# Joins of phases in a one-core graph kernel: the first head's rows kept on chip, row statistics taken at the close of a layer, graph products in pairs of groups

## The chip, the cores and the metric

The kernel runs on one core of a Trainium2 chip. The metric is the device time of one execution in microseconds (us). Every run that is quoted here is in the fast of the two states in which executions can fall. The engines are called as the profile calls them: PE (matrix products), PEld (loads of PE's stationary operand), DVE (VectorE), ACT (ScalarE), POOL (GpSimd), SP (the engine that issues most transfers). A name with a q is an engine's sequencer or its transfer queue.

## The reference

4096 nodes with 256 features; `adj` is a symmetric 0/1 matrix with ones on its diagonal. Layer 0 is graph attention with 4 heads, layer 1 two steps of a diffusion. Cut to what matters:

```python
def layer0(x, adj, W, a, gamma, beta):            # on relu(layernorm(x))
    h = (x @ W).reshape(n, heads, head_dim)
    e = leaky_relu(src[:, :, None] + dst.T[None])  # rank one per head, alpha 0.2
    attn = softmax(where(adj > 0, e, -9e15))
    out = einsum('nhm,mhd->nhd', attn, h)
    return layernorm(out) * gamma + beta

def layer1(X, S, ...):                            # on relu(layernorm(x)), S = adj
    R = (S + I) / rowsum
    for n in range(2):
        A = top_p_attention(Xa)                    # softmax rows cut to their 0.9 nucleus
        Xf, Xa = R @ Xf, A @ Xa
        Z = Z + Xf @ U1[n].T + Xa @ U2[n].T
    return layernorm(X + Z) * ln_g + ln_b

x = x + layer0(relu(layernorm(x)), adj, ...)
x = x + layer1(relu(layernorm(x)), adj, ...)
```

In this case's inputs gamma and ln_g are ones, and beta and ln_b are zeros. The kernel does not use that.

## The kernel before

Five phases follow each other. (1) The operand phase: per block of 128 rows the layer norm, x @ W, and bf16 operands for all heads, which are stored to DRAM. (2) Sixteen attention passes, four groups of eight row blocks times four heads: signs on ACT, masks on DVE, products on PE; a pass of the first head follows each group, and in it and in the pass before it eight row blocks are "closed" (normalised, gamma, beta, x). (3) The rows are read back, normalised and split in two for exact products with adj ("hops": R @ Xf, twice). (4) The first and (5) the second diffusion step, 32 row blocks each, software-pipelined over several blocks: exponentials on ACT, a search for the nucleus' threshold on DVE and POOL, transposes and products on PE. Last comes a repair of the rows that the fast search did not settle.

The parts that the change touches:

```python
# (1) operand phase, per group g of four row blocks
for i in range(4):
    ...
    nc.scalar.dma_start(uv_d[:, :, b].rearrange("h p t w -> p h t w"), parts)
for i in range(4):
    nc.gpsimd.tensor_tensor(x4[:, i, :], x4[:, i, :], beta_r, ALU.add)
nc.sync.dma_start(xb_d[ts(g, 4)].rearrange("b p d -> p b d"), x4)
# ... [cut]
# (2) closing of row block b
def close(i):
    b = ig * G0 + i
    xb = l0s.tile([P, D], F32, name="xb")
    nc.sync.dma_start(xb, xb_d[b])
    ob = l0s.tile([P, D], F32, name="ob")
    nc.scalar.activation(ob, o[:, i, :], AF.Identity, scale=..., bias=...)
    nc.vector.tensor_mul(ob, ob, gamma_r)
    nc.vector.tensor_add(xb, xb, ob)
    nc.sync.dma_start(x1_d[b], xb)
# ... [cut]
# (3) rows back, then one group of four row blocks after the other
for g in range(NB // 4):
    nc.scalar.dma_start(X[:, ts(g, 4), :], x1_d[ts(g, 4)].rearrange("b p d -> p b d"))
    for i in range(4):
        moments_of(mv[:, i, :], X[:, 4 * g + i, :])
    rs, nmr = steps(mv, 4, rr)
    for i in range(4):
        nc.scalar.activation(X[:, b, :], X[:, b, :], AF.Relu, scale=rs[:, i:i + 1], bias=nmr[:, i:i + 1])
        split(hl[0][:, b], X[:, b, :])
# ... [cut]
# (5) end of a row block in the second step
nc.gpsimd.tensor_tensor(r.x1, r.x1, ln_b_r, ALU.add)
nc.vector.tensor_add(hb, r.acc[:, 1, :], r.part)
normalized(hb, hb)            # DVE moments, POOL rs = (var + eps) ** -0.5, DVE rows
nc.vector.tensor_mul(hb, hb, ln_g_r)
nc.vector.tensor_add(hb, hb, r.x1)
# ... [cut]  the order in which one turn of the pipeline is traced
second_probe(blocks[b + 1])   # a pass of DVE over 4096 columns, then a chain on POOL
candidates(r, found)          # DVE
first_step(blocks[b + 2])     # a chain on POOL
third_probe(blocks[b + 1])    # a pass of DVE over 4096 columns
finish(blocks.pop(b - 2))     # the lines above
masked(r)                     # a pass of DVE over 4096 columns
```

## Time and profile before

| what | kernel before |
|---|---|
| time | 3629.36 us, median of 3 runs (3628.36 to 3630.86) |
| span of the profiled run, mean granted clock | 3626.4 us, 0.928 |
| busy share PE, PEld, DVE, ACT, POOL | 85, 68, 76, 55, 33% |
| first masks / last evacuation of the attention passes | 160.07 / 956.18 us |
| first graph product / end of the last group of them | 999.59 / 1473.67 us |
| turn of the pipeline in the second step | 28.21 to 28.23 us |

How to read it: most engines are busy in the mean, but no engine bounds the whole. What a change is worth is read from the joins, where all engines wait for one thing, and from the steady turns, where the longest engine's cycle counts. "First masks" is the start of ACT's first sign operation in the attention passes; "last evacuation" is the start of the last time that ACT takes a pass's sums from PE's accumulators. One turn of the pipeline finishes one row block, and a "probe" is one of DVE's passes over 4096 columns. In all views a line of instructions has its start, its length, the engine and line of the program, the operation, out<-in with shapes, and in brackets how long the engine had been idle before and what ended that.

### The profile page before, as it was taken

What the parts mean: (1) busy time and instruction counts of PE and PEld (TensorE: products, weight loads), DVE (VectorE), ACT (ScalarE), POOL (GpSimd) and SP (SyncE); (2) the same over time, 40 slices, a digit from 0 to 9 for tenths busy, and PEclk for the clock granted to TensorE, in tenths of its full rate; (3) what the DMA queues carried; (4) which work ended last, traced back from release to release, by engine and by line L of the source; (5) the groups of instructions that cost most, each with busy time, mean ns of one, the idle gap of its engine ahead of it and who ended that gap; (6) DMA issues with size and microseconds to landing.
All of it is one profiled execution on the core that took longest, in us unless ns stands there. A gap on an engine that the chain in (4) does not pass through costs nothing. (4 is left out here: it accounts for less than half of the span.)

```text
span 3626.4 us, 52748 instructions
## 1 busy us (share of the span) xinstructions
PE 3073.0 (85%) x19243; PEld 2460.8 (68%) x19243; DVE 2745.2 (76%) x5073; ACT 2008.7 (55%) x3180; POOL 1193.6 (33%) x2236
## 2 busy tenths in 40 slices
PE   4499898989599999848999999998489999999973
PEld 2399797989578888625676767685266666666762
DVE  6589898989665555229999999971399999899963
ACT  4588786878431100266666666633666666666521
POOL 3100000000010000048897554530475555555510
PEclk7699999999899999969999999999689999999986
DMA  9827456382154545100000000001000000000002
GB/s 274 259 84 195 163 143 210 94 234 76 49 175 163 163 163 164 45 1 9 17 15 18 15 17 15 17 18 56 1 11 21 18 18 18 23 19 18 18 20 29
DMA packets 212144, 278.26 MB, mean 77 GB/s; under 512 B 18720, under 2 KB 168864, under 8 KB 211872
## 3 DMA queue, kind: packets, MB, share of 16 engines
q1 hardware_dynamic: 162416, 214.45, 18.2%
q0 software_dynamic: 16896, 33.56, 5.1%
q10 hardware_dynamic: 32560, 26.75, 2.3%
q8 instruction: 157, 2.57, 0.3%
q14 instruction: 115, 0.94, 0.1%
HBM read 230.16 MB, written 78.09 MB: 85 GB/s over the span
## 5 line engine op out<-in xcount | busy, mean ns | idle before, releaser
L768 PE MATMUL acc<-X,eT 128*128 128x256 f32 x4160 | 999.9, 384 | 27.2 <-ACT eT L762 27.2
L768 PEld LDWEIGHTS acc<-X,eT 128*128 128x128 f32 x4160 | 761.1, 191 | 148.1 <-ACT eT L762 61.0
L281 PE MATMUL acc<-ut,m 128*128 128x195 bf16 (+1 forms) x8192 | 729.6, 249 | 84.8 <-DVE m L269 40.8
L281 PEld LDWEIGHTS <-m 128*128 128x128 bf16 x8192 | 703.3, 98 | 111.0 <-DVE m L269 56.5
L262 ACT ACTIVATE g<-sr,d_big 128x1024 bf16<-128x1024 f32 x512 | 550.2, 1178 | 50.2 <-DVE m L268 36.9
L611 ACT ACTIVATE void<-e,c 128x2048 int8<-128x2048 f32 x256 | 516.3, 2017 | 1.0
L423 PE MATMUL racc<-hl,ar 128*128 128x512 f32 x2048 | 470.0, 392 | 45.8 <-DMA at<-adj_d 41.1
L604 ACT ACTIVATE e<-mm,nm 128x1024 f32<-128x1024 f32 x256 | 284.0, 1112 | 385.7 <-PE mm L466 385.4
L423 PEld LDWEIGHTS racc<-hl,ar 128*128 128x128 f32 x2048 | 387.4, 189 | 128.2 <-POOL nmr L136 41.3
L760 PE MATMUL tp<-ident,e 128*128 128x128 f32 x2080 | 329.3, 285 | 154.9 <-DVE e L698 120.3
L760 PEld LDWEIGHTS tp<-ident,e 128*128 128x128 f32 x2080 | 251.9, 145 | 285.6 <-issue 152.1
L762 ACT COPY eT<-tp 128x512 f32<-128x512 f32 x520 | 304.1, 587 | 215.4 <-PE tp L760 215.4
L268 DVE TENSOR_TENSOR m<-g,ax 128x2048 bf16<-128x2048 bf16 x256 | 312.0, 1219 | 46.3 <-ACT g L262 42.7
L677 DVE MAX8 cand<-big 128x8 f32<-128x256 f32 x1024 | 340.3, 409 | 0.0
L466 PE MATMUL mm<-kT,qT 64*128 64x512 f32 x1024 | 286.5, 663 | 62.5 <-ACT e L604 52.1
L269 DVE TENSOR_TENSOR m<-ax,m 128x2048 bf16<-128x2048 bf16 x256 | 313.6, 1225 | 26.2 <-DVE m L268 0.5
L645 DVE SCALAR_TENSOR_TENSOR junk<-e,lowered 128x4096 uint8<-128x4096 f32 x64 | 286.1, 4471 | 55.9 <-POOL lowered L627 55.9
L419 DVE CAST ar<-at 128x1024 fp32r<-128x1024 bf16 x256 | 177.3, 693 | 192.4 <-PE racc L423 187.4
L666 DVE SCALAR_TENSOR_TENSOR big<-e,lowered 128x4096 f32<-128x4096 f32 x64 | 286.7, 4480 | 16.0 <-POOL lowered L627 16.0
L698 DVE SCALAR_TENSOR_TENSOR e<-e,found 128x4096 f32<-128x4096 f32 x64 | 286.7, 4480 | 0.0
L432 ACT ACTIVATE xf<-xf,rinv 128x256 f32<-128x256 f32 x64 | 32.7, 510 | 392.4 <-DVE xf L431 392.4
L466 PEld LDWEIGHTS mm<-kT,qT 64*128 64x128 f32 x1024 | 87.7, 196 | 177.6 <-issue 96.1
(230 smaller groups left out, 3288.4 us busy)
## 6 DMA issues: line engine op xcount, KB each, us to landing
at<-adj_d SPq DMA_DIRECT2D x256, 256.0 KB, 2.8
ut<-uv_d SPq DMA_DIRECT2D x64, 784.0 KB, 4.3
ax<-in_adj_t_dram POOLq DMA_DIRECT2D x32, 1024.0 KB, 13.5
adj_d<-ax SPq DMA_DIRECT2D x32, 1024.0 KB, 11.1
uv_d<-parts ACTq DMA_DIRECT2D x32, 392.0 KB, 9.6
xf<-xf_d SPq DMA_DIRECT2D x65, 128.0 KB, 2.0
sr<-s_d SPq DMA_DIRECT2D x16, 512.0 KB, 4.8
xf_d<-xf ACTq DMA_DIRECT2D x64, 128.0 KB, 2.2
```

Source lines behind the costliest of these rows:

```text
L262: nc.scalar.activation(g[:, c, :], shared[k].sr, AF.Relu, scale=BIG, bias=d_big[:, h, j:j + 1])
L268: nc.vector.tensor_tensor(m[0], g, a, ALU.min)
L269: nc.vector.tensor_tensor(m[1], a, m[0], ALU.subtract)
L281: nc.tensor.matmul(shared[k].acc[i][:, t, :cols], m[t][:, c, ts(i, P)], shared[k].ut[j // QUARTER][:, j % QUARTER, t, :cols], start=(j == ...
L423: nc.tensor.matmul(acc[i].rearrange("p s d -> p (s d)"), ar[:, c, ts(i, P)], hl[hop][:, j].rearrange("p s d -> p (s d)"), start=(j == 0), ...
L466: nc.tensor.matmul(pm[:, h, :], q[ts(h, DA), :], kT[ts(h, DA), ts(c, 512)], start=True, stop=True)
L611: nc.scalar.activation(void, r.e[:, ts(h, N // 2)], (AF.Relu, AF.Sign)[i], bias=r.c1, scale=-1.0, accum_out=r.sums[:, h, 2 + i:3 + i])
L666: nc.vector.scalar_tensor_tensor(big, r.e, r.c3, r.e, ALU.is_le, ALU.mult, accum_out=r.L)
L677: nc.vector.max(cand[:, s, :], big[:, ts(s, N // SEG)])
L760: nc.tensor.transpose(pt[:, i, :], r.e[:, ts(4 * g + i, P)], ident)
L762: nc.scalar.copy(eT, pt)
L768: nc.tensor.matmul(r.acc[:, 0, :], eT[:, i, :], cur[:, j, :], start=(j == 0), stop=(j == NB - 1))
```

## The change

Its intent is to close the holes between phases: fewer bytes and no reload at the first join; the statistics of finished rows early, so that they can be read back and used while the last eight blocks are closed; and two groups of graph products that take the rows of those eight blocks last. In the second step the normalisation is cut in three pieces, spread over two turns.

```diff
-            beta_r = row_vector(beta, "beta_r", l0w)
+    beta_r = row_vector(beta, "beta_r")              # gamma_r likewise: no longer in layer 0's memory
...
+        ut0 = [quarter() for q in range(4)]          # pool of these tiles opened before the operand phase
...
+                    nc.gpsimd.tensor_copy(ut0[b // QUARTER][:, b % QUARTER], parts[:, 0])
                     nc.scalar.dma_start(uv_d[:, :, b].rearrange("h p t w -> p h t w"), parts)
-                for i in range(4):
-                    nc.gpsimd.tensor_tensor(x4[:, i, :], x4[:, i, :], beta_r, ALU.add)
-                nc.sync.dma_start(xb_d[ts(g, 4)].rearrange("b p d -> p b d"), x4)
...
-                    nc.sync.dma_start(xb, xb_d[b])
+                    nc.sync.dma_start(xb, x[ts(b, P), :])
...
                     nc.vector.tensor_mul(ob, ob, gamma_r)
+                    nc.gpsimd.tensor_tensor(xb, xb, beta_r, ALU.add)
                     nc.vector.tensor_add(xb, xb, ob)
                     nc.sync.dma_start(x1_d[b], xb)
+                    moments_of(mv[:, i, :], xb)
+                    if i == G0 - 1:
+                        steps(mv, G0, l0s, x_rs[:, ts(ig, G0)], x_nmr[:, ts(ig, G0)])
...
-            mv = rr.tile([P, 4, nc.vector.BN_AGGR_DIM], F32, name="mv4", bufs=2)
-            for i in range(4):
-                moments_of(mv[:, i, :], X[:, 4 * g + i, :])
-            rs, nmr = steps(mv, 4, rr)
...
+            for ig in range(0, NB // IG, 2):
+                accs = [[psr.tile(...) for i in range(IG)] for g in range(2)]
+                late = (NB - G0) // JG if ig == 0 else NB // JG
+                for first, last in ((0, late), (late, NB // JG)):
+                    for g in range(2):
+                        part(hop, ig + g, accs[g], first, last)
+                        if last == NB // JG:
+                            close_rows(hop, ig + g, accs[g])
+                    if ig > 0:
+                        break
...
                 if b + 2 < NB:
                     first_step(blocks[b + 2])
+                if b > 2:
+                    finish_scale(blocks[b - 3])      # POOL: x1 + ln_b, then the two operations of rs
                 if b + 1 < NB:
                     third_probe(blocks[b + 1])
                 if b > 1:
-                    finish(blocks.pop(b - 2))
+                    finish(blocks[b - 2])            # DVE: sum and moments
+                if b > 2:
+                    finish_rows(blocks.pop(b - 3))   # DVE: rows, ln_g, x1
                 masked(r)
```

Cut: pools and names, the reload of the first 24 row blocks put on SP's queue instead of ACT's, the loops of the graph products moved into two functions, the calls in the repair and at the end (three blocks' pieces together).

More of the change, by code (lines that the diff above doesn't have):

```diff
@@ L98, in gat_then_top_p_diffusion @@
     ln_b_r = row_vector(ln_b, "ln_b_r")
+    gamma_r = row_vector(gamma, "gamma_r")
+    beta_r = row_vector(beta, "beta_r")
     w31_s = const.tile([P, KC, 3, DA], F32, name="w31_s")
@@ L107, in gat_then_top_p_diffusion @@
             nc.scalar.dma_start(w2_s[ts(j, DA), i, :], w2_t)
-    rinv = keep.tile([P, NB], F32, name="rinv")
+    rinv, x_rs, x_nmr = (keep.tile([P, NB], F32, name=x) for x in ("rinv", "x_rs", "x_nmr"))
     xa_d = dram.tile([NB, P, D], F32, name="xa_d")
@@ L129, in normalized, with steps @@
         nc.vector.tensor_scalar(dst, src, mv[:, 0:1], rs, ALU.subtract, ALU.mult)
-    def steps(mv, n, pool):
-        rs, nmr = (pool.tile([P, n], F32, name=x, bufs=2) for x in (f"rs{n}", f"nmr{n}"))
+    def steps(mv, n, pool, rs=None, nmr=None):
+        if rs is None:
+            rs, nmr = (pool.tile([P, n], F32, name=x, bufs=2) for x in (f"rs{n}", f"nmr{n}"))
         nc.gpsimd.tensor_scalar(rs, mv[:, :, 1], EPS, None, ALU.add)
@@ L153, in gat_then_top_p_diffusion @@
     s_d = dram.tile([H, N], F32, name="s_d")
-    xb_d = dram.tile([NB, P, D], F32, name="xb_d")
     adj_d = dram.tile([NB, P, N], BF16, name="adj_d")
-    with tc.tile_pool(name="l0", bufs=1) as l0, tc.tile_pool(name="l0a", bufs=9) as l0a:
-        gamma_r = row_vector(gamma, "gamma_r", l0)
+    with tc.tile_pool(name="l0", bufs=1) as l0, tc.tile_pool(name="l0a", bufs=9) as l0a, \
+            tc.tile_pool(name="l0u", bufs=6) as l0u:
         sd_c = l0.tile([P, 2, H, NB], F32, name="sd_c")
@@ L169, in gat_then_top_p_diffusion, with quarter @@
         ax = []
+        QUARTER = NB // 4
+        def quarter():
+            return l0u.tile([P, QUARTER, 2, W3 + 1], BF16, name="ut")
+        ut0 = [quarter() for q in range(4)]
         with tc.tile_pool(name="l0r", bufs=3) as rows, tc.tile_pool(name="l0w", bufs=1) as l0w, \
                 tc.tile_pool(name="ps2", bufs=2, space=PSUM) as ps2:
-            beta_r = row_vector(beta, "beta_r", l0w)
             a_r = row_vector(a, "a_r", l0w)
@@ L232, in gat_then_top_p_diffusion @@
                 nc.scalar.activation(e, e, AF.Exp)
-        with tc.tile_pool(name="l0m", bufs=3) as l0m, tc.tile_pool(name="l0u", bufs=6) as l0u, \
+        with tc.tile_pool(name="l0m", bufs=3) as l0m, \
                 tc.tile_pool(name="l0s", bufs=2) as l0s, tc.tile_pool(name="l0o", bufs=1) as l0o, \
@@ L237, in gat_then_top_p_diffusion @@
             PAIRS = NB // 2
-            QUARTER = NB // 4
             passes = [(ig, h) for ig in range(NB // G0) for h in range(H)]
@@ L251, in weighted @@
             def weighted(k, q):
-                ut = l0u.tile([P, QUARTER, 2, W3 + 1], BF16, name="ut")
+                ut = quarter()
                 nc.sync.dma_start(ut, uv_d[passes[k][1], :, ts(q, QUARTER)])
@@ L348, in sign_stage @@
                         sources(0)
-                        weighted(0, 0)
-                        weighted(0, 1)
+                        shared[0].ut = ut0
                     gs[n] = signs(k, p)
@@ L359, in mask_stage @@
                         nq = k * 4 + p // 4 + 2
-                        if nq < 4 * len(passes):
+                        if 4 <= nq < 4 * len(passes):
                             if nq % 4 == 0:
@@ L391, in gat_then_top_p_diffusion @@
     X = xp.tile([P, NB, D], F32, name="X")
-    with tc.tile_pool(name="rx", bufs=1) as rx, tc.tile_pool(name="ra", bufs=3) as ra, \
-            tc.tile_pool(name="rr", bufs=1) as rr, tc.tile_pool(name="psr", bufs=2, space=PSUM) as psr:
+    with tc.tile_pool(name="rx0", bufs=1) as rx0, tc.tile_pool(name="ra", bufs=3) as ra, \
+            tc.tile_pool(name="rr", bufs=1) as rr, tc.tile_pool(name="rx1", bufs=1) as rx1, tc.tile_pool(name="psr", bufs=2, space=PSUM) as psr:
         def split(dst, src):
@@ L399, in split @@
             nc.vector.tensor_tensor(dst[:, 1, :], src, dst[:, 0, :].bitcast(F32), ALU.subtract)
-        hl = [rx.tile([P, NB, 2, D], F32R, name=f"hl{i}") for i in range(2)]
+        hl = [rx.tile([P, NB, 2, D], F32R, name=f"hl{i}") for i, rx in enumerate((rx0, rx1))]
         for g in range(NB // 4):
-            nc.scalar.dma_start(X[:, ts(g, 4), :], x1_d[ts(g, 4)].rearrange("b p d -> p b d"))
-            mv = rr.tile([P, 4, nc.vector.BN_AGGR_DIM], F32, name="mv4", bufs=2)
-            for i in range(4):
-                moments_of(mv[:, i, :], X[:, 4 * g + i, :])
-            rs, nmr = steps(mv, 4, rr)
+            (nc.sync if g < 6 else nc.scalar).dma_start(X[:, ts(g, 4), :], x1_d[ts(g, 4)].rearrange("b p d -> p b d"))
@@ L408, in gat_then_top_p_diffusion @@
             for i in range(4):
                 b = 4 * g + i
-                nc.scalar.activation(X[:, b, :], X[:, b, :], AF.Relu, scale=rs[:, i:i + 1], bias=nmr[:, i:i + 1])
+                nc.scalar.activation(X[:, b, :], X[:, b, :], AF.Relu, scale=x_rs[:, b:b + 1], bias=x_nmr[:, b:b + 1])
                 split(hl[0][:, b], X[:, b, :])
-        for hop in range(STEPS):
-            for ig in range(NB // IG):
-                acc = [psr.tile([P, 2, D], F32, name=f"racc{i}") for i in range(IG)]
-                for jg in range(NB // JG):
-                    at = ra.tile([P, JG, IG * P], BF16, name="at", bufs=6)
-                    nc.sync.dma_start(at, adj_d[ts(jg, JG), :, ts(ig, IG * P)].rearrange("c p i -> p c i"))
-                    ar = ra.tile([P, JG, IG * P], F32R, name="ar")
-                    nc.vector.tensor_copy(ar, at)
-                    for c in range(JG):
-                        j = jg * JG + c
-                        for i in range(IG):
-                            nc.tensor.matmul(acc[i].rearrange("p s d -> p (s d)"), ar[:, c, ts(i, P)],
-                                             hl[hop][:, j].rearrange("p s d -> p (s d)"),
-                                             start=(j == 0), stop=(j == NB - 1))
-                for i in range(IG):
-                    b = ig * IG + i
-                    both = rr.tile([P, 2, D], F32, name="both")
-                    nc.vector.tensor_tensor(both, acc[i], hl[hop][:, b].bitcast(F32), ALU.add)
-                    xf = rr.tile([P, D], F32, name="xf")
-                    nc.vector.tensor_tensor(xf, both[:, 0, :], both[:, 1, :], ALU.add)
-                    nc.scalar.activation(xf, xf, AF.Copy, scale=rinv[:, b:b + 1])
-                    nc.scalar.dma_start(xf_d[hop][b], xf)
-                    if hop + 1 < STEPS:
-                        split(hl[hop + 1][:, b], xf)
@@ new lines, in part @@
+        def part(hop, ig, acc, first, last):
+            for jg in range(first, last):
+                at = ra.tile([P, JG, IG * P], BF16, name="at", bufs=6)
+                nc.sync.dma_start(at, adj_d[ts(jg, JG), :, ts(ig, IG * P)].rearrange("c p i -> p c i"))
+                ar = ra.tile([P, JG, IG * P], F32R, name="ar")
+                nc.vector.tensor_copy(ar, at)
+                for c in range(JG):
+                    j = jg * JG + c
+                    for i in range(IG):
+                        nc.tensor.matmul(acc[i].rearrange("p s d -> p (s d)"), ar[:, c, ts(i, P)],
+                                         hl[hop][:, j].rearrange("p s d -> p (s d)"),
+                                         start=(j == 0), stop=(j == NB - 1))
@@ new lines, in close_rows @@
+        def close_rows(hop, ig, acc):
+            for i in range(IG):
+                b = ig * IG + i
+                both = rr.tile([P, 2, D], F32, name="both")
+                nc.vector.tensor_tensor(both, acc[i], hl[hop][:, b].bitcast(F32), ALU.add)
+                xf = rr.tile([P, D], F32, name="xf")
+                nc.vector.tensor_tensor(xf, both[:, 0, :], both[:, 1, :], ALU.add)
+                nc.scalar.activation(xf, xf, AF.Copy, scale=rinv[:, b:b + 1])
+                nc.scalar.dma_start(xf_d[hop][b], xf)
+                if hop + 1 < STEPS:
+                    split(hl[hop + 1][:, b], xf)
@@ new lines, in gat_then_top_p_diffusion @@
+        for hop in range(STEPS):
+            for ig in range(0, NB // IG, 2):
+                accs = [[psr.tile([P, 2, D], F32, name=f"racc{i}") for i in range(IG)] for g in range(2)]
+                late = (NB - G0) // JG if ig == 0 else NB // JG
[6 more added lines that the diff above has]
+                        break
@@ L748, in loads @@
     def loads(r):
-        r.xf, r.part = rows.tile([P, D], F32, name="xf"), rows.tile([P, D], F32, name="part")
+        r.xf, r.part = rows.tile([P, D], F32, name="xf"), rows.tile([P, D], F32, name="part", bufs=3)
         nc.sync.dma_start(r.xf, block(xf_d[r.n], r.b))
@@ L752, in loads @@
             nc.sync.dma_start(r.part, block(z_d, r.b))
-            r.x1 = rows.tile([P, D], F32, name="x1")
+            r.x1 = rows.tile([P, D], F32, name="x1", bufs=3)
             nc.sync.dma_start(r.x1, block(x1_d, r.b))
@@ L843, in again @@
         finish(r)
+        finish_scale(r)
+        finish_rows(r)
     def repaired(n, kT, qT, nm, cur, found):
@@ L895, in finish, with finish_scale, finish_rows @@
         else:
-            nc.gpsimd.tensor_tensor(r.x1, r.x1, ln_b_r, ALU.add)
-            hb = rows.tile([P, D], F32, name="hb", bufs=1)
-            nc.vector.tensor_add(hb, r.acc[:, 1, :], r.part)
-            normalized(hb, hb)
-            nc.vector.tensor_mul(hb, hb, ln_g_r)
-            nc.vector.tensor_add(hb, hb, r.x1)
-            nc.sync.dma_start(block(out.rearrange("(b p) d -> b p d", p=P), r.b), hb)
+            nc.vector.tensor_add(r.part, r.acc[:, 1, :], r.part)
+            r.mv = small.tile([P, 1, nc.vector.BN_AGGR_DIM], F32, name="mv1")
+            moments_of(r.mv[:, 0, :], r.part)
+    def finish_scale(r):
+        if r.n + 1 == STEPS:
+            nc.gpsimd.tensor_tensor(r.x1, r.x1, ln_b_r, ALU.add)
+            r.rs = col("rs")
+            nc.gpsimd.tensor_scalar(r.rs, r.mv[:, :, 1], EPS, None, ALU.add)
+            nc.gpsimd.tensor_tensor(r.rs, r.rs, mhalf, ALU.pow)
+    def finish_rows(r):
+        if r.n + 1 == STEPS:
+            nc.vector.tensor_scalar(r.part, r.part, r.mv[:, 0, 0:1], r.rs, ALU.subtract, ALU.mult)
+            nc.vector.tensor_mul(r.part, r.part, ln_g_r)
+            nc.vector.tensor_add(r.part, r.part, r.x1)
+            nc.sync.dma_start(block(out.rearrange("(b p) d -> b p d", p=P), r.b), r.part)
     for n in range(STEPS):
@@ L947, in gat_then_top_p_diffusion @@
             finish(r)
+            for b in range(NB - 3, NB):
+                finish_scale(blocks[b])
+            for b in range(NB - 3, NB):
+                finish_rows(blocks[b])
         repaired(n, kT, qT, nm, cur, found)
```

## The prediction

> **What bounds the kernel now.** I read the page, then the busy time by stretch, then the time-ordered instructions at each join of two phases. The page gives a span of 3626.4 us with PE 85% busy, so no single engine explains it; the stretches do. (Columns: stretch, length, busy us of PE, PEld, DVE, ACT, POOL, then granted PE clock, DMA share, GB/s.)
>
> ```profile
> 10.00:150.00 140.00, 67.55 (x193) 43.11 (x193) 86.39 (x235) 70.83 (x196) 48.11 (x101) 0.71 1.04 284
> 163.00:956.00 793.00, 727.04 (x8165) 701.00 (x8166) 700.19 (x723) 630.74 (x774) 30.16 (x35) 0.98 0.49 141
> 958.00:1000.00 42.00, 0.94 (x8) 0.73 (x6) 19.94 (x61) 11.29 (x27) 5.32 (x11) 0.56 0.40 127
> 2634.00:3500.00 866.00, 777.98 (x3747) 584.53 (x3747) 788.94 (x1674) 508.31 (x756) 468.16 (x984) 0.95 0.06 19
> ```
>
> The first stretch, where layer 0's operands are made, is full on DMA (share 1.04) with DVE at 62%. The second, the attention passes, has PE and DVE both near 90%. The third is a hole: PE works 0.94 us of 42. The last is the second diffusion step, with DVE at 91%. The waits of the first stretch say what DMA holds up: a new operand buffer is not free until an old one's store has landed.
>
> ```profile
> POOL parts L211 <- DMA uv_d<-parts: 64.3, 17, 7.6
> ```
>
> Next the two joins, in order of time (start, length, engine, line, out<-in, count, idle before it and what ended that):
>
> ```profile
> 149.16 0.37 ACTq L219 DMA_DIRECT2D uv_d<-parts  x1
> 160.07 5.30 ACT L262 ACTIVATE g<-sr,d_big 128x1024 bf16<-128x1024 f32 x5 [11.78 <-DMA uv_d<-parts]
> ...
> 163.67 0.32 PE L281 MATMUL acc<-ut,m 128*128 128x196 bf16 x1 [19.52 <-DMA ut<-uv_d]
> ```
>
> ```profile
> 961.35 1.78 DVE L300 TENSOR_TENSOR st<-st 128x1560 f32<-128x1560 f32 x1 [8.01 <-ACT st L296]
> ...
> 987.62 2.70 ACTq L403 DMA_DIRECT2D X<-x_d  x4
> ...
> 999.59 1.62 PE L423 MATMUL racc<-hl,ar 128*128 128x512 f32 x3 [41.06 <-DMA at<-adj_d]
> ```
>
> First join: the last store, issued at 149.16, lands only near 160, and the first masks wait for it. Second join: DVE and ACT close the last eight row blocks from 961 to 988; only then are the rows read back, normalised and split, and PE starts at 999.6.
>
> **What the Trainium skill says.** (1) "SBUF — State Buffer", section "SBUF: two separate sides": VectorE and GpSimd share a port pair under an exclusive lock; a VectorE operation with two SBUF inputs, against a GpSimd operation that reads SBUF, holds it for its whole length. The trace of before agrees: below, a POOL operation that elsewhere takes 0.26 us takes 4.02 under the 4.48 us probe. (2) "DMA: Bandwidth & Descriptors", section "Issuing engines are not separate DMA queues": all queues run on the same 16 DMA engines. The full share of the first stretch with 64.3 us of waiting for stores agrees, so a store taken off one queue helps another. (3) "TensorE: Matmul & The Clock Gate", section on the HAM clock gate: after idling PE starts at half rate for some microseconds. Here the first eight graph products take 3.75 us, 0.47 each, and 443 per 100 us (0.226 each) later.
>
> **The change, part by part.**
>
> *First head's rows on chip, and no copy of x plus beta in DRAM.* Gone from the first stretch: eight stores of 512 KB (4.2 MB). Over its first 100 us this queue moved 12.65 MB in 38.2% of the 16 engines' time, 3.0 us per MB, so 12.7 us of DMA. On POOL 32 additions of 0.73 us go and 32 copies of about that come, a wash. With the share at 1.04 and the compute of a block (2.1 to 2.4 us between blocks near 34 to 40 us, against 3.7 on average) well below it, I take 10 of the 12.7. At the first join four loads of 784 KB of the first head are gone; three of them were in flight with the last store. That store should land in 5 us rather than 11: 6 more. The masks still wait for it, so not all 11.8. Sum -16.
>
> *Row statistics at the close of layer 0.* Each close gets a bn_stats and a bn_aggr on DVE. In the second step the same pair behind an add starts its parts 0.46 us apart, so about 0.67 us per block. The passes that close rows are DVE-bound: the pass from 346.45 to 410.66 (64.2 us between evacuations, 46.1 elsewhere) has 52.4 us of DVE work plus 11.6 of DVE waits, nearly all of it, while PE idles 11. So 24 closes x 0.67 = +16 there. About 4.6 is given back, because DVE now arrives later at waits such as this one, whose end is fixed by a DMA queue that stands behind another transfer:
>
> ```profile
> 397.50 0.42 DVE L335 TENSOR_TENSOR xb<-xb,ob 128x256 f32<-128x256 f32 x1 [6.01 <-DMA xb<-xb_d]
> ```
>
> The addition of beta on POOL (0.73 us, later if DVE holds the ports) now follows such a load: +3 to 4 over three closings. Sum +15.
>
> *The second join.* Rows 0 to 23 were stored long before, and their statistics now exist. Their loads need only X's memory, free after the last evacuation (961.3; gamma, which kept it until 987.6, has moved). A first load took 4.3 us (987.62 to 991.96), then relu, cast and split take about 2: PE starts near 968, 32 earlier. That asks that ACT and DVE take this work between the closing's instructions. The order of before allows it: in this view an instruction traced after the second step's blocks (L850) stands inside the last block's search:
>
> ```profile
> 3494.55 0.19 DVE L691 TENSOR_SCALAR work<-drop 128x48 f32<-128x48 f32 x1
> 3494.65 0.18 DVE L850 TENSOR_TENSOR failed<-found,found 128x32 f32<-128x32 f32 x1
> 3494.77 0.21 DVE L692 CUSTOM_DVE_ANT_0 work<-best,work 128x48 f32<-128x48 f32 x1
> ```
>
> ACT makes a block in 0.9 us (relu 0.55, cast 0.35), the pace at which PE eats one (4 x 0.226). DVE has 0.72 us per block (split 0.37, half a cast 0.35) beside 20 us of closing, 37 us from 965, so the first group's 24 blocks end near 1000. The second group's 24 (21.7 us) follow at full rate and cover the last eight rows. Then 1000 + (2048 - 96) x 0.226 = 1441, against 1474 in before: -33. Two groups that end 7.2 us apart need their accumulators emptied at about 3.1 us per block, so the third group waits 1 to 2 us in each hop: +3. Sum -30.
>
> *The normalisation of the second step in three pieces.* This is meant to take away DVE's wait of 1.84 us per block, some 29 blocks, 53 us. I think it takes nothing:
>
> ```profile
> 3020.13 4.48 DVE L666 SCALAR_TENSOR_TENSOR big<-e,lowered 128x4096 f32<-128x4096 f32 x1
> 3020.72 4.02 POOL L627 TENSOR_SCALAR lowered<-lowered,c 128x1 f32<-128x1 f32 x1
> ...
> 3024.70 0.19 POOL L639 TENSOR_TENSOR yy<-a 128x1 f32<-128x1 f32 x1
> 3024.85 0.55 POOL L640 TENSOR_TENSOR up<-z,mone 128x1 f32<-128x1 f32 x1
> 3025.45 0.18 DVE L124 BATCH_NORM_AGGREGATE mv<-st 128x2 f32<-128x6 f32 x1
> 3025.50 0.26 POOL L641 TENSOR_SCALAR up<-up,sg 128x1 f32<-128x1 f32 x1
> 3025.71 0.73 POOL L896 TENSOR_TENSOR x<-x,ln_b_r 128x256 f32<-128x256 f32 x1
> 3026.53 0.25 POOL L126 TENSOR_SCALAR ve<-mv 128x1 f32<-128x1 f32 x1
> 3026.87 0.57 POOL L128 TENSOR_TENSOR rs<-ve,mhalf 128x1 f32<-128x1 f32 x1
> 3027.47 0.41 DVE L129 TENSOR_SCALAR hb<-hb,mv,rs 128x256 f32<-128x256 f32 x1 [1.84 <-POOL rs L128]
> ```
>
> POOL is locked out during the probe and then runs the rest of the step's arithmetic, the addition of ln_b, and the two operations of rs without a pause. The moments are ready at 3025.63, 0.9 us before POOL reaches them at 3026.53: they aren't what it waits for. The change makes the moments a block older but leaves POOL's order (arithmetic, addition, two operations) and DVE's order (three, three, mask) as they were, so rs still comes 2.9 us after the probe and DVE still waits 1.84. The period of 28.23 us stays: 0. At the end three blocks' rows are finished together behind one chain on POOL: +1.6.
>
> Total: -16 + 15 - 30 + 0 + 1.6 = -29, so 3629.4 - 29 = 3600 us.
>
> **Rivals.** *The split normalisation works.* For: it names the longest regular wait on DVE, and PE's own cycle is 26.19 us (step one's steady period), so DVE's 26.39 would count. Against: POOL's unbroken row above. It would make 3629 - 29 - 53, about 3547. *The second join isn't interleaved*: ACT and DVE finish the closing first. For: the closing was written in a fixed order. Against: L850. PE would then start near 989 and the change would give about 3620. *The first stretch doesn't shrink*, if the buffers' round trip and not the bytes sets its pace: about 3610. *DVE in the passes hides the statistics*: no PE or DVE slack speaks for it; 3585.
>
> **Range and chances.** My terms are uncertain by 7 (first stretch), 6 (passes) and 10 us (second join), 14 together: 3572 to 3624 holds it 8 times in 10. Over 2% faster is below 3557, which needs the first rival: 0.09. Within 2%: 0.9. Slower by over 2% has no source that I can see: 0.01.
>
> **What would show it.** In the changed kernel: first masks near 144; no xb_d store; the passes with closings 4 to 5 us longer; first graph product near 967 (968, moved by the -16 and +15 of the first two terms) POOL, not DMA, ahead of some xb additions; the last graph product some 30 us earlier relative to the closing; in the second step a DVE wait of about 1.8 us for POOL's rs in every block at a period of 28.2. If that period is 26.4, the step "POOL's order sets rs" is wrong, and with it the total.

## The result, and the profile after

The changed kernel takes 3600.27 us, median of 4 runs (3595.79 to 3604.97), against 3630.11 (3628.36 to 3631.09); ratio 0.9918, 95% interval 0.9901 to 0.9936. A ratio here is the mean time of one kernel's fast runs over that of the other's of the same rounds, so not quite the ratio of the medians quoted. The result is correct in all runs.

The time came out where it was predicted, with a range that held it. Whether the reasons were right is another question. The first profile happens to be of the slowest of the four runs, so the account below uses two profiles (the second is that of the experiment after_again).

Busy time by stretch, the stretches that answer to three of those of before (stretch, length, busy us of PE, PEld, DVE, ACT, POOL, granted clock, DMA share, GB/s):

```profile
10.00:142.00 132.00, 64.71 (x193) 41.30 (x193) 82.99 (x232) 69.33 (x193) 43.47 (x99) 0.75 1.01 274
156.00:954.00 798.00, 730.34 (x8161) 701.30 (x8162) 719.03 (x770) 630.48 (x773) 67.02 (x71) 0.98 0.48 137
2611.00:3475.00 864.00, 772.09 (x3759) 580.67 (x3760) 790.37 (x1673) 507.80 (x755) 477.04 (x984) 0.96 0.06 19
```

The operand phase is still full on DMA (1.01). In the passes DVE has 19 us more work than before and POOL 37. The second step looks the same: 790 us of DVE work there, 789 before.

The first join, in order of time:

```profile
145.16 0.37 ACTq L227 DMA_DIRECT2D uv_d<-parts  x1
152.46 1.15 ACT L266 ACTIVATE g<-sr,d_big 128x1024 bf16<-128x1024 f32 x1 [8.17 <-DMA uv_d<-parts]
```

The last store is issued 4.0 us earlier than before and is waited for 7.3 us after its issue, where it was 10.9. The second join:

```profile
959.68 1.78 DVE L304 TENSOR_TENSOR st<-st 128x1560 f32<-128x1560 f32 x1 [8.00 <-ACT st L300]
...
967.78 1.62 PE L426 MATMUL racc<-hl,ar 128*128 128x512 f32 x3 [10.93 <-issue]
```

PE starts the graph products 8 us after DVE begins the last closing (38 us before).

What DVE waited for in the passes (engine, what for, us in total, times, longest), from the view of waits from 250 to 960 us. Before:

```profile
DVE xb L335 <- DMA xb<-xb_d: 16.7, 4, 7.8
```

After:

```profile
DVE xb L340 <- POOL xb L339: 1.2, 2, 0.6
```

One turn of the second step, after:

```profile
2994.05 3.98 POOL L645 TENSOR_SCALAR lowered<-lowered,c 128x1 f32<-128x1 f32 x1
...
2999.01 0.74 POOL L923 TENSOR_TENSOR x<-x,ln_b_r 128x256 f32<-128x256 f32 x1
...
2999.84 0.25 POOL L925 TENSOR_SCALAR rs<-mv 128x1 f32<-128x1 f32 x1
3000.18 0.57 POOL L926 TENSOR_TENSOR rs<-rs,mhalf 128x1 f32<-128x1 f32 x1
...
3000.78 0.41 DVE L930 TENSOR_SCALAR part<-part,mv,rs 128x256 f32<-128x256 f32 x1 [1.85 <-POOL rs L926]
```

DVE waits 1.85 us for rs, as it did before, although the moments that rs needs are now a whole turn old. The turn is 28.21 to 28.24 us.

The account, from the starts of instructions in the profiled runs (us, after minus before):

| stretch | predicted | first profile | second profile |
|---|---|---|---|
| start to first masks | -16 | -7.6 | -6.3 |
| first masks to last evacuation (796.1 before) | +15 | +5.9 | +5.8 |
| last evacuation to end of the graph products (517.5) | -30 | -29.0 | -26.9 |
| projections, up to the first masked block of step one (171.5) | 0 | +5.9 | +1.1 |
| from there to the last masked block of step two (1853.6) | 0 | -4.3 | -5.8 |
| tail with the repair (127.7) | +1.6 | +5.8 | +6.2 |
| sum | -29 | -23 | -26 |

### The profile page after: what moved, and what is told of

Same layout as the page of the kernel before. It is cut to its first block, busy times and chain, and to the rows that moved or that the text cites. A ratio compares the mean times of both kernels' runs of the same rounds, so it can differ in the third digit from the quotient of the medians.

```text
span 3603.2 us, 52704 instructions
## 1 busy us (share of the span) xinstructions
PE 3070.6 (85%) x19243; PEld 2455.2 (68%) x19243; DVE 2753.2 (76%) x5073; ACT 2008.2 (56%) x3180; POOL 1237.2 (34%) x2252
## 5 line engine op out<-in xcount | busy, mean ns | idle before, releaser
L285 PEld LDWEIGHTS <-m 128*128 128x128 bf16 x8192 | 703.9, 98 | 112.8 <-DVE m L273 65.6
L426 PE MATMUL racc<-hl,ar 128*128 128x512 f32 x2048 | 470.6, 391 | 16.3 <-issue 10.9
```

The costliest lines, as they stand in the source:

```text
L285: nc.tensor.matmul(shared[k].acc[i][:, t, :cols], m[t][:, c, ts(i, P)], shared[k].ut[j // QUARTER][:, j % QUARTER, t, :cols], start=(j == ...
L426: nc.tensor.matmul(acc[i].rearrange("p s d -> p (s d)"), ar[:, c, ts(i, P)], hl[hop][:, j].rearrange("p s d -> p (s d)"), start=(j == 0), ...
```

## The experiments

Twelve runs were made; all gave correct results. Each was timed against the kernel before in the same rounds. Where a difference lies below the spread of the times (the changed kernel's runs spread over 9 us), the verdict is taken from the starts of instructions in the trace, one profile each.

| run | us, median | ratio to before (95%) |
|---|---|---|
| pool_first | 3550.17 | 0.9781 (0.9768 to 0.9794) |
| no_add | 3574.03 | 0.9846 (0.9832 to 0.9859) |
| split_alone | 3628.59 | 0.9995 (0.9982 to 1.0009) |
| rs_before_add | 3628.45 | 0.9996 (0.9980 to 1.0013) |
| stats_alone | 3628.30 | 0.9996 (0.9982 to 1.0010) |
| no_beta_add | 3594.50 | 0.9897 (0.9880 to 0.9913) |
| store_back | 3608.24 | 0.9944 (0.9927 to 0.9960) |
| reload_head | 3601.65 | 0.9918 (0.9901 to 0.9934) |
| both_back | 3607.82 | 0.9934 (0.9917 to 0.9950) |
| one_group | 3615.93 | 0.9956 (0.9940 to 0.9973) |
| stats_at_reload | 3615.51 | 0.9957 (0.9941 to 0.9974) |
| after_again | 3602.37 | 0.9919 (0.9902 to 0.9936) |

The kernel before had medians of 3630.51 (the first four: pool_first, no_add, split_alone, stats_alone), 3631.26 (store_back, reload_head, one_group, no_beta_add) and 3631.04 (the others). The first four ran on another chip than the other eight; these medians show no difference between the two.

### The second step: does POOL's order set rs?

**pool_first.**

```diff
+                if b > 2:
+                    finish_scale(blocks[b - 3])
                 if b + 2 < NB:
                     first_step(blocks[b + 2])
-                if b > 2:
-                    finish_scale(blocks[b - 3])
                 if b + 1 < NB:
                     third_probe(blocks[b + 1])
```

> The changed kernel with one move: GpSimd's three operations for the final normalisation (the addition of ln_b and the two of rs) are traced before the first search step of the block after next, and not behind it. Theory of the prediction (GpSimd's order sets rs: it is locked out by the probe and has its arithmetic ahead of rs): rs is ready before the probe, VectorE's wait of 1.84 us per block in the second step goes, the period falls from 28.23 to about 26.4 us, and 29 blocks x 1.84 = 53 us less than the changed kernel: about 3547 us, 0.977 of the kernel before. Rival (the moments, or a wait of the program that does not depend on the order, hold the rows up): period stays 28.2, 3600 us. Second rival: the arithmetic of the search then comes 1.6 us later, and its result is waited for: period between 27 and 28.

Measured: 3550.17 us. The turn is 26.33 to 26.35 us, and the view of what DVE waited for between 2700 and 3350 us has no line left. One turn, in order of time:

```profile
2985.48 0.73 POOL L923 TENSOR_TENSOR x<-x,ln_b_r 128x256 f32<-128x256 f32 x1
...
2986.30 0.24 POOL L925 TENSOR_SCALAR rs<-mv 128x1 f32<-128x1 f32 x1
...
2986.62 0.57 POOL L926 TENSOR_TENSOR rs<-rs,mhalf 128x1 f32<-128x1 f32 x1
...
2988.11 4.48 DVE L684 SCALAR_TENSOR_TENSOR big<-e,lowered 128x4096 f32<-128x4096 f32 x1
...
2988.14 4.62 POOL L654 TENSOR_SCALAR L<-L,c,sums 128x1 f32<-128x1 f32 x1
```

The operations for rs end 0.9 us before the probe begins. What the probe now locks out (an operation of about 0.4 us that lasts 4.62) is the arithmetic of a block two turns ahead, for which nobody waits yet. This is the theory's prediction to within 0.1 us of the turn and 3 us of the time, so the step "POOL's order sets rs" is shown. It also beats both kernels.

**no_add.**

```diff
-            nc.gpsimd.tensor_tensor(r.x1, r.x1, ln_b_r, ALU.add)
```

> The changed kernel without GpSimd's addition of ln_b (right all the same, as ln_b is zero in this case's inputs), order unchanged. Theory (rs waits behind a queue of work on GpSimd that starts when the probe ends): the queue is 0.8 us shorter, so VectorE's wait falls from 1.84 to about 1.0 us and the period from 28.23 to 27.4 us, 24 us less than the changed kernel, about 3577. Rival (rs waits for the moments or for a semaphore round trip): nothing changes, 3600.

Measured: 3574.03 us. The wait totals 27.1 us in 24 turns between 2700 and 3350 us, 1.1 each; the turn is 27.51 us. So rs stands behind a queue: 0.8 us less of it, 0.7 us less waiting. Of the 26 us against the changed kernel the second step gives 20 (from its first to its last masked block 838.5 us in place of 858.5), the tail the rest.

**split_alone.** The kernel before with only the three pieces (the last hunk of the diff above, and buffers).

> The kernel before with nothing but the normalisation of the second step in three pieces. Theory: 0 +- 3 us against the kernel before (3627 to 3633), with the wait of 1.84 us and the period of 28.23 us standing, plus 1 to 2 us at the end. Rival (the split helps and another part of the change takes it back): 40 to 53 us faster.

Measured: 3628.59, ratio 0.9995. The turn is 28.21, and the wait of DVE for rs is 43.3 us in 23 turns, 1.9 each. The split alone is worth nothing, as the theory said. It is what makes pool_first possible: the rows' moments have to be a turn old before POOL can be asked for rs ahead of the probe.

**rs_before_add.** The kernel before, with one line moved:

```diff
-            nc.gpsimd.tensor_tensor(r.x1, r.x1, ln_b_r, ALU.add)
             hb = rows.tile([P, D], F32, name="hb", bufs=1)
             nc.vector.tensor_add(hb, r.acc[:, 1, :], r.part)
             normalized(hb, hb)
+            nc.gpsimd.tensor_tensor(r.x1, r.x1, ln_b_r, ALU.add)
```

> The kernel before with one line moved: in the final normalisation GpSimd's addition of ln_b is traced behind its two operations for rs. Theory (a queue on GpSimd ahead of rs): 0.73 us less ahead of rs, as the moments are ready 0.9 us before GpSimd gets to it, so VectorE's wait falls from 1.84 to 1.1 us, the period from 28.23 to 27.5, 21 us less than the kernel before: about 3609, 0.994. Rival (the moments' chain through the semaphores sets the wait): no change.

A miss: 3628.45 us instead of 3609. The wait did fall as expected, to 26.3 us in 23 turns (1.1 each). But the turn is 27.97 to 28.00 and not 27.5:

```profile
3026.53 0.73 POOL L899 TENSOR_TENSOR x<-x,ln_b_r 128x256 f32<-128x256 f32 x1
3026.59 0.81 DVE L129 TENSOR_SCALAR hb<-hb,mv,rs 128x256 f32<-128x256 f32 x1 [1.15 <-POOL rs L128]
```

The addition now starts 0.06 us ahead of the instruction that had waited for rs, and in every turn that one takes 0.81 us where it took 0.41. Of the 0.69 us won 0.39 go there, and 0.07 in a wait before the second instruction after it. This looks like the lock of the Trainium skill, page "SBUF — State Buffer", section "SBUF: two separate sides", seen from the other side: whichever starts first has the ports. The page binds the lock to the kind of DVE instruction; whether this one (one tensor and two columns of scalars) is of that kind no run here shows. I had reckoned with the lock against POOL only. The remaining 0.24 us a turn are there in the trace: from its first to its last masked block the second step takes 857.6 us, 863.9 before, and the spans of the four runs have a median of 3622.95 us against 3629.15. The time doesn't show it, because in each of these runs it is 5.0 to 5.9 us longer than the span, and 1.8 to 1.9 in those of the kernel before. Why stays open.

### The attention passes: what do statistics and additions cost?

**stats_alone.** The kernel before with the statistics at the close, unused:

```diff
                     nc.sync.dma_start(x1_d[b], xb)
+                    moments_of(mv[:, i, :], xb)
+                    if i == G0 - 1:
+                        steps(mv, G0, l0s, x_rs[:, ts(ig, G0)], x_nmr[:, ts(ig, G0)])
```

> The kernel before with the row statistics computed at each close of layer 0 and not used (the reload computes its own as before). It measures that cost by itself. The prediction's step: 24 closes x 0.67 us = 16 us in the attention passes, less 4.6 absorbed by transfers: the last evacuation 11 us later, and 8 x 0.67 = 5 us more in the last closing: 3641 to 3646. Rival (most of it falls into waits of VectorE, as the changed kernel's passes suggest, which took 5.9 us more in all): the last evacuation 4 to 6 us later, 3635 to 3641.

Both missed: 3628.30 us, no difference. From first masks to last evacuation it takes 797.6 us (796.1 before), although the instructions are there: 24 bn_stats of 0.428 us and as many bn_aggr of 0.182 us, 14.6 us of DVE. What made room is in the waits of DVE from 250 to 960 us:

```profile
DVE xb L336 <- DMA xb<-xb_d: 0.5, 1, 0.5
```

Of the 16.7 us that DVE had waited for transfers of xb, 16.2 are gone. SP's queue shows why. In the first closing before (the wait of 6.01 us that the prediction shows was for the second of these):

```profile
392.25 0.37 SPq L366 DMA_DIRECT2D adj_d<-ax  x1
393.26 0.96 SPq L331 DMA_DIRECT2D xb<-xb_d  x1
```

and the same load of xb here:

```profile
387.83 0.32 SPq L332 DMA_DIRECT2D xb<-xb_d  x1
```

Before, SP's queue stood 6.4 us at the store of an adjacency tile whose own load, issued by POOL at 383.88 us, had not landed; the load of xb stood behind it. Here the statistics' operations stand ahead of that load in POOL's queue. It is issued at 429.95 us, after the closing, and its store is out of the way of xb. The second closing shows the same (588 and 633 us); the third has no such load. So the statistics did not only fill these waits: in two closings, 13.8 of the 16.7 us, they took away the cause, by their place in POOL's queue. This is read from the times of issue; no run moved that load alone. The three closing passes go from 64.2, 65.6 and 60.8 us to 62.3, 62.2 and 62.0, and the pass after each takes 1.4 us more. In the last closing, from last evacuation to first graph product, it costs 44.4 instead of 43.4 us.

**no_beta_add.** The changed kernel without this line:

```diff
-                    nc.gpsimd.tensor_tensor(xb, xb, beta_r, ALU.add)
```

> The changed kernel without GpSimd's addition of beta in the closings of layer 0 (right all the same: beta is zero in these inputs). Prediction's step: these additions cost 3 to 4 us over three closings because they follow the load. What the traces suggest instead: they slow VectorE's own instructions (masks 1226 to 1259 ns, products with gamma 420 to 488 ns) by about 1.6 us per closing: the closing passes go from 63.9 to 62.2 us, 5 us in the three, as in the run with the statistics alone; last evacuation 5 us earlier relative to the first masks, whole about 5 us faster. Rival (the passes' pace has another cause): 63.9 stays.

Measured: 3594.50 us, 6 to 8 us less than the two medians of the changed kernel. The closing passes go from 63.9 us to 62.3, 62.2 and 61.9, the stretch of all passes from 802.1 to 796.9. Groups of DVE instructions between 330 and 460 us (line, operation, shapes, count, busy us, mean ns, idle before), in the changed kernel:

```profile
L273 DVE TENSOR_TENSOR m<-ax,m 128x2048 bf16<-128x2048 bf16 x38 | 47.6, 1254 | 3.8
...
L338 DVE TENSOR_TENSOR ob<-ob,gamma_r 128x256 f32<-128x256 f32 x8 | 3.9, 488 | 2.8 <-ACT ob L337 2.8
```

and without the addition:

```profile
L273 DVE TENSOR_TENSOR m<-ax,m 128x2048 bf16<-128x2048 bf16 x39 | 47.8, 1225 | 3.9
...
L338 DVE TENSOR_TENSOR ob<-ob,gamma_r 128x256 f32<-128x256 f32 x8 | 3.4, 420 | 2.8 <-ACT ob L337 2.8
```

The addition is hardly waited for (1.2 us in all three closings). It costs by making DVE's own instructions longer: 29 ns each of 38 masks is 1.1 us, 68 ns each of 8 products 0.5, so 1.6 us per closing. That the sum of three is 5 us is measured. The single instructions of the changed kernel from 330 to 960 us confirm it: of 195 masks of this line the eight that began during an addition took 1.56 to 1.63 us, no other over 1.23; four products with gamma that began during one took 0.95 to 0.98 us, no other over 0.43. With one mask of the other line (1.75; three of it that began in the last 0.1 us of an addition kept their 1.2) that is 5.6 us more in all. Instructions that had begun before the addition kept their length, and so did the statistics' instructions, which read one tensor. That the ports are the reason is inferred from this.

### The second join: which part carries it?

**one_group.**

```diff
-                late = (NB - G0) // JG if ig == 0 else NB // JG
-                for first, last in ((0, late), (late, NB // JG)):
+                late = NB // JG
+                for first, last in ((0, late),):
```

> The changed kernel with the graph products in one group after the other, as before, everything else kept. If the pairing is what covers the last eight rows: the first group reaches row block 24 near 995 and waits for the rows, which in the changed kernel are split between 1011 and 1020; first two groups end near 1051 in place of 1036, so 12 to 15 us slower than the changed kernel, about 3613. Rival (without the second group's casts the last rows are ready much sooner, so the early start alone carries the gain): 0 to 4 us slower.

Measured: 3615.93 us, 14 to 16 more than the two medians of the changed kernel. From last evacuation to the end of the graph products it takes 501.3 us, where the changed kernel took 488.5 and 490.6. PE, in order of time:

```profile
997.81 2.14 PE L426 MATMUL racc<-hl,ar 128*128 128x512 f32 x8 [0.62 <-DVE hl L406]
1012.85 6.19 PE L426 MATMUL racc<-hl,ar 128*128 128x512 f32 x16 [12.90 <-DVE hl L406]
```

The first group starts as early as in the changed kernel, runs out of rows near 1000 and waits 12.9 us for the last eight blocks. That wait is what the second group fills.

**stats_at_reload.** The statistics back at the reload, the rest of the change kept:

```diff
-                    moments_of(mv[:, i, :], xb)
-                    if i == G0 - 1:
-                        steps(mv, G0, l0s, x_rs[:, ts(ig, G0)], x_nmr[:, ts(ig, G0)])
...
+            mv = rr.tile([P, 4, nc.vector.BN_AGGR_DIM], F32, name="mv4", bufs=2)
+            for i in range(4):
+                moments_of(mv[:, i, :], X[:, 4 * g + i, :])
+            steps(mv, 4, rr, x_rs[:, ts(g, 4)], x_nmr[:, ts(g, 4)])
```

> The changed kernel with the row statistics taken when the rows are read back, as in the kernel before, everything else kept (the early start, the two groups). It shows what their early place is worth at the second join. Theory: the last closing's VectorE gets 24 x 0.6 = 15 us of statistics that now stand between load and first product, less 5 us of its own eight rows: the first graph product 3 to 5 us later after the last evacuation (13.3 us in the changed kernel), the products' end 8 to 12 us later; in the attention passes nothing comes back or at most 5 us, as the statistics lay mostly in transfer waits: 3603 to 3612 in all. Rival (early statistics don't matter, the order of groups carries the join): within 3 us of the changed kernel, or faster.

Slower than expected: 3615.51 us. The first graph product comes 24.0 us after the last evacuation (13.3 in the changed kernel), and the next ones run dry:

```profile
969.90 7.17 PE L427 MATMUL racc<-hl,ar 128*128 128x512 f32 x20 [21.66 <-issue]
...
992.62 8.09 PE L427 MATMUL racc<-hl,ar 128*128 128x512 f32 x24 [14.09 <-DVE ar L423]
```

To the end of the products it takes 513.1 us, 23 to 25 more than the changed kernel; only 4 of the join's gain are left. The passes give 9.9 back (792.0 us), more than the 5 I allowed. So early statistics are the larger part of the join; the two groups are worth 11 to 13 on top of them.

### The first stretch: bytes, or what else?

**store_back.** Eight stores of 512 KB again, of the plain input rows:

```diff
                     nc.scalar.dma_start(uv_d[:, :, b].rearrange("h p t w -> p h t w"), parts)
+                nc.sync.dma_start(xb_d[ts(g, 4)].rearrange("b p d -> p b d"), x4)
```

> The changed kernel with eight stores of 512 KB put back into the first stretch (the input rows into an unused array, no addition), which are the bytes that the change took off the DMA engines there. The prediction's step (the stretch is bound by bytes, 4.2 MB x 3.0 us = 12.7 us, of which 10 count): first masks near 162 instead of 152.5, the whole 10 us slower than the changed kernel. What the changed trace suggests (the last store was issued 4.0 us earlier and landed 3.6 us sooner): first masks near 156 to 160, 4 to 7 us slower. Rival (the round trip of the operand buffers or the loads of the adjacency set the pace, not the bytes): first masks stay within 2 us of 152.5.

**reload_head.** No `ut0`; the first head's quarters are loaded from DRAM:

```diff
-                    nc.gpsimd.tensor_copy(ut0[b // QUARTER][:, b % QUARTER], parts[:, 0])
...
-                        shared[0].ut = ut0
+                        weighted(0, 0)
+                        weighted(0, 1)
...
-                        if 4 <= nq < 4 * len(passes):
+                        if nq < 4 * len(passes):
```

> The changed kernel with the first head's rows read back from DRAM as before (no copies on GpSimd in the first stretch, four loads of 784 KB at the join). Prediction's step: these loads compete with the last store and cost 6 us at the join: first masks 6 us later than 152.5. Rival: the masks wait for that store alone and its landing does not depend on them: within 2 us; or the 32 copies on GpSimd and the buffers they hold cost as much as they save: faster by 1 to 4 us.

**both_back.** Both edits together.

> The changed kernel with both parts of the first stretch undone: the eight stores of 512 KB are back, and the first head's rows are read back from DRAM (no additions of beta on GpSimd there). Alone, the stores moved the first masks from 152 to 156.3, the loads from 152 to 150.5. If the two add up: first masks at 154 to 156. If the loads compete with the last store only when the other stores are there too (the prediction's mechanism at the join, with bytes as the limit): 159 to 160, as in the kernel before.

The first masks, and the time from the issue of the last store of operands to them:

| kernel | first masks, us | after the last store's issue, us |
|---|---|---|
| four with before's first stretch | 159.3 to 160.3 | 10.7 to 11.2 |
| seven with the changed one | 149.8 to 153.9, mean 152.6 | 7.2 to 7.4 |
| store_back | 156.3 | 7.3 |
| reload_head | 150.5 | 7.9 |
| both_back | 158.4 | 7.3 |

The stores' bytes are worth about 4 us here, not 10 (one profile, against a mean whose seven values spread over 4 us). Reading the first head's rows back shows no cost by itself. But both_back is no undoing of that part: its tiles still come from a pool that is opened ahead of the operand phase, and its trace has three of the four loads at 73, 102 and 138 us, as the quarters are done. In before the tiles shared memory with the operand phase, and three of the loads were issued from 146.98 us on, beside the last store, the fourth at 159.9. What shortened the landing by 3.5 us is thus the place of the pool, and keeping the rows on chip was not needed for it. This is argued from the times of issue; a kernel with the pool alone moved did not run. Together the stores and the loads are worth 6 of the 7; the last 1 to 2 us lie within the spread of first masks.

### Chance in one profile

**after_again.** The changed kernel, unchanged.

> The changed kernel once more, for a second profile in its ordinary state: its first profile was the slowest of its four runs, with a granted clock of 0.74 instead of the 0.83 to 0.87 of all other kernels in the 40 us of projections that follow the graph products. If that was chance, those 40 us are at 0.83 to 0.87 here, the first search step starts 172 to 175 us after the last graph product and not 177, and the time is 3596 to 3603. If it belongs to the change, 0.74 and 177 come again.

Measured: 3602.37 us. The 40 us after the graph products, in the first profile and in this one (columns as above):

```profile
1443.00:1483.00 40.00, 28.69 (x114) 17.96 (x114) 5.74 (x11) 12.42 (x24) 0.15 (x1) 0.74 0.10 30
```

```profile
1446.00:1486.00 40.00, 28.12 (x133) 17.60 (x132) 6.16 (x12) 14.23 (x27) 0.15 (x1) 0.83 0.10 30
```

At a granted clock of 0.74 PE got 114 products done, at 0.83 133 of them in the same 40 us. The first masked block comes 172.6 us after the end of the graph products, not 177.4. So some 5 us of the first profile were chance and are no part of the change. The same comes once more in the profile of both_back (0.74, 177.7 us); in the other seven variants of the changed kernel it is 0.83 to 0.87.

## Why the prediction was right, and where it was not

The total (-29) and the class were right, and so were the two steps with the largest stakes. Two terms were mis-sized, by about 9 us each in opposite directions, and cancelled: that the total fell on 3600 is luck in that part.

**Split normalisation, 0: right, and by the reason given.** The turn stayed at 28.2 and the wait at 1.85 us; the lines above have POOL's row in the order that the prediction read from before. pool_first, no_add and split_alone agree with the theory, and the rival (3547 us) needed only the order that the change did not take. What failed near it was my use of the same lock for rs_before_add.

**Second join, -30: right.** -29.0 and -26.9. The first graph product came 13.3 and 13.0 us after the last evacuation, where 968 - 956.2 = 11.8 was foretold; that it stands at 967.78 us (967 foretold) owes something to the two earlier errors, which cancel there. ACT and DVE do take the early rows between the closing's instructions, so the rival without interleaving (3620) is out. The term of +3 for emptying two groups' accumulators was too large: in the second hop the third group's sum is taken at 1297.95 us where 1210.47 and three times the group of 29.01 make 1297.50.

**First stretch and first join, -16: the sign right, the size not.** -7.6 and -6.3. The term that failed is "I take 10 of the 12.7": the bytes are worth about 4, by store_back. A share of 1.04 says that the DMA engines were full, not that each byte taken off comes back as time; blocks still waited for buffers (56.5 us after, 64.3 before) and for the adjacency's loads. The term of 6 at the join measured 3.5.

**Attention passes, +15: the sign right, the size not.** +5.9 and +5.8. The step that failed is "About 4.6 is given back". It took the transfer behind which xb's load stands as fixed, and counted one wait of 6.01 us where the view of waits had 16.7. With statistics or additions ahead of it in POOL's queue the adjacency's load came later (384 us before, 430 in stats_alone, 404 in stats_at_reload), SP's queue was free ahead of xb, and most of that wait went. The profiles can then be read as one sum. The passes without that block would take about 787 us, an estimate: 792.0 with additions alone (stats_at_reload) plus 796.9 with statistics alone (no_beta_add) less 802.0 with both. On these 787 the statistics cost 10, where 16 - 4.6 = 11 was predicted, and the additions 5, where 3 to 4 was. The missing term is the 9 us that the kernel before lost to the blocked queue (796.1). The sum has as many terms as these four profiles, so it can't fail; beside it stand stats_alone with 797.6, 5.6 us of lengthened instructions for the additions, and 13.8 us of waits for the block. No run removed the block alone: it is a reading and not a test. The rival that I put aside, that DVE in the passes hides the statistics, had the size for the kernel before (1.5 us in stats_alone), but not this reason. The additions cost what they do by lengthening DVE's instructions, not by following a load. A slip without consequence: the 52.4 us of DVE work in the pass from 346.45 us is PE's column of that view; DVE's is 50.3.

**Tail, +1.6: nearly right as a sum.** The second step's last masked block comes 4 to 6 us earlier, as the normalisation of one block more now stands behind it, and the tail is 6 us longer: together +0.4 to +1.5. Some 2 us of the tail are the three blocks' pieces at its head. Up to 4 us lie in the repair, between instructions that wait for branches and small loads; in no_add the tail is 127.7 us, as before, and in split_alone 131.5. This was not resolved.

## What to carry to other kernels

Work on a second engine that stands in one queue has to be placed by when the queue is locked or busy, not by when its inputs are ready: the same three instructions were worth 0 behind a locked stretch and some 50 us in front of it. A wait for a transfer is as fixed as what stands ahead of that transfer in its queue: here new operations on POOL moved another load, and with it went most of 17 us of waiting. So before adding a cost to a busy engine sum the whole view of its waits, not one of them, and follow each through the queue. And when a total comes out right, check its terms: here two were off by about 9 us each and hid one another.

## What the Trainium skill lacked or had wrong

- "SBUF — State Buffer", section "SBUF: two separate sides", says that of two that contend for the shared ports the second is fully blocked. For each order of issue the page gives one ratio, without the lengths of the instructions. Here POOL operations of 0.26 to 0.38 us took 4.0 to 4.6 us under a 4.48 us VectorE probe, which agrees. The other way, an addition of 0.73 us on POOL that had started 0.06 us earlier made a VectorE instruction of 0.41 us last 0.81: 0.40 us more, less than the 0.67 us that were left of the addition (spans on POOL are rough). Masks of 1.23 us that began during an addition took 1.56 to 1.63, products of 0.42 us took 0.95 to 0.98.
- The pages state the lock and the order of an engine's queue apart; none says what the first does to the work behind the locked instruction. Here it held up all that POOL had been given, and what VectorE waited for in each turn (1.84 us, 53 in the step) was the arithmetic left for after the probe, not the locked operation itself.
- "TensorE: Matmul & The Clock Gate", section on the HAM clock gate, says that the ramp depends on the run and is small against a kernel's span. That fits, if the ramp is what differed: the same 40 us of one kernel had a granted clock of 0.74 and of 0.83 in two runs, some 5 us of 3600. The page doesn't point out that for a change worth 30 us this is a sixth, so that one profile is too few.
